# Mixture of experts in float32: tokens held in the array, or weights held in the array

## The chip, the cores and the metric

The kernel runs on one core of a Trainium2 chip. A core has TensorE (matrix products, with a separate instruction that loads the operand held in the array), VectorE, ScalarE, GpSimd and SyncE, which all run side by side and meet at semaphores, and 16 DMA engines that move data between the chip's main memory and the on-chip memory. TensorE writes its products to a small memory of banks (PSUM), from which VectorE and ScalarE read. The metric is the time of one execution on the device in microseconds (us), median of several runs. All data is float32.

## What is computed

Four layers run one after the other over an image batch `x` of shape (2, 128, 56, 56), each added to its input: agent attention, a 3x3 convolution, a mixture of experts over patches, and a pair of recurrent (Mamba) blocks. Only the third is touched:

```
xp = patches of the normalized x          # 1568 tokens of d = 512
probs = softmax(xp @ router_w)            # 8 experts
topv, topi = top_k(probs, 2)              # the two best, shares sum to 1
for e in range(8):
    h = xp @ w1[e]                        # w1[e]: 512 x 2048
    val, g = split(h, 2)                  # 1024 each
    he = val * sigmoid(g)
    out = out + gate[:, e:e+1] * (he @ w2[e])   # w2[e]: 1024 x 512
```

The kernel computes an expert only for the tokens that chose it.

## The kernel before, in words

**Routing.** `PatchExperts.route` finds the two experts of each token, sorts the 3136 pairs by expert, and pads each expert's pairs to whole tiles of 128 slots (`SLOTS`). The tokens lie in main memory as rows of 512 (`xd`). For the inputs shown here 28 tiles come out. `whom` holds the token of each slot, `whose` the expert of each tile, `share` the weight of each slot.

**One tile.** `PatchExperts.run` (line 1298) works through the tiles `j`. `gather(j)` fetches the tile's 128 token rows with an indirect DMA from GpSimd's queue into `xr` (four buffers). `up_weights` and `down_weights` (lines 1314 and 1319) bring the expert's two matrices, 4 MB and 2 MB, through SyncE's queue, each into one of two buffers, used in turn.

`up(j, w1, xr)` (line 1327) turns the token rows: four transposes on TensorE into a PSUM bank (`xr_ps`, line 1331) and one copy by VectorE (`xs_c`, line 1333), so that the 512 features lie on partitions as four blocks of 128, with the 128 tokens along the free axis. Then the first layer: for each half `c` of the 1024 inner features and each part (1, the gate; then 0, the value) four matmuls accumulate over the four feature blocks (line 1341). The token block `xc[:, q, :]` is held in the array and 512 columns of the matrix stream past it, so a row of the result is a token:

```
nc.tensor.matmul(h_ps, xc[:, q, :], w1[:, q, f0 : f0 + 512], start=q == 0, stop=q == 3)
```

ScalarE takes the sigmoid of the gate (`sg`, line 1344), VectorE multiplies (`he`, line 1345).

`down(j, he, w2)` (line 1348) computes the second layer. It sums over the 1024 inner features, so these must lie on partitions: eight transposes turn `he` in two banks (`he_ps`, line 1354), ScalarE copies the first to `ht` (line 1357), VectorE the second (line 1359). Then eight matmuls with 512 streamed columns accumulate `o_ps` (line 1362), ScalarE scales each row by its share (`ot`, line 1364) and sends it to `os` in main memory (line 1365).

**Order of the work.** The loop emits `up` of a tile before `down` of the tile before, and a scheduler with the pools' buffers as its limits decides each engine's final order. On TensorE a tile then reads: `xr` transposes, first four `he` transposes of the tile before, 16 matmuls of `h`, other four `he` transposes, eight matmuls of `o` of the tile before. PSUM has four buffers for `h`, two for the transposes (`xr_ps` and `he_ps` share them) and two for `o`. SyncE's queue is in order: the second-layer matrix for tile `j + 2` waits for `o` of tile `j`, and behind it stands the first-layer matrix for tile `j + 3`. The first 25 tiles are unrolled; for the rest a switch on the number of further tiles has one branch for each number, and three tiles are run there.

**Around it.** `combine` (line 1394) gathers each token's two result rows once the last `os` has landed, turns them and adds them to `x`; the recurrent stage starts from there.

Of the kernel before, what the change touches and what calls it, by code (L numbers as in the profile page):

```python
# [8 lines left out]
F32 = mybir.dt.float32  # L9
# [8 lines left out]
P = 128  # L18
# [991 lines left out]
SLOTS = 128  # L1010
# [3 lines left out]
class PatchExperts:  # L1014
# [283 lines left out]
    def run(self, wpool, work, ps):  # L1298
        net, nc, a = self.net, self.net.nc, self.net.a
        experts, hidden, toks = self.experts, self.hidden, self.toks  # L1300
        nj = hidden // P

        w1s = a["L2_conv_w1"].rearrange("e (c q) f -> e c q f", q=4)
        w2s = a["L2_conv_w2"].rearrange("e (j k) d -> e k j d", k=P)

        def expert(j):
            return bass.ds(nc.sync.value_load(self.whose[0:1, j : j + 1], min_val=0, max_val=experts - 1), 1)

        ups = [wpool.tile([P, 4, 2 * hidden], F32, name="w1", tag="w1") for _ in range(2)]
        downs = [wpool.tile([P, nj, 512], F32, name="w2", tag="w2") for _ in range(2)]  # L1310

        def up_weights(j, e):
            w1 = ups[j % 2]
            nc.sync.dma_start(w1, w1s[e].rearrange("o c q f -> (o c) q f"))
            return w1

        def down_weights(j, e):
            w2 = downs[j % 2]
            nc.sync.dma_start(w2, w2s[e].rearrange("o k j d -> (o k) j d"))
            return w2  # L1320

        def gather(j):
            xr = work.tile([SLOTS, 512], F32, name="xr", tag="xr", bufs=4)
            self.rows_of(xr, self.xd, self.whom[:, j : j + 1], toks)
            return xr

        def up(j, w1, xr):

            tp = ps.tile([P, 512], F32, name="xr_ps", tag="tr")
            for q in range(4):  # L1330
                nc.tensor.transpose(tp[:, q * P : (q + 1) * P], xr[:, q * P : (q + 1) * P], net.ident)  # L1331
            xc = work.tile([P, 4, SLOTS], F32, name="xs_c", tag="xs_c")
            nc.vector.tensor_copy(xc.rearrange("c q s -> c (q s)"), tp)
            he = work.tile([SLOTS, hidden], F32, name="he", tag="he")
            for c in range(2):
                parts = []
                for part in (1, 0):
                    h_ps = ps.tile([P, 512], F32, name="h_ps", tag="h", bufs=4)
                    f0 = part * hidden + c * 512
                    for q in range(4):  # L1340
                        nc.tensor.matmul(h_ps, xc[:, q, :], w1[:, q, f0 : f0 + 512], start=q == 0, stop=q == 3)  # L1341
                    parts.append(h_ps)
                sg = work.tile([SLOTS, 512], F32, name="sg", tag="sg")
                nc.scalar.activation(sg, parts[0], AF.Sigmoid)  # L1344
                nc.vector.tensor_mul(he[:, c * 512 : (c + 1) * 512], parts[1], sg)  # L1345
            return he

        def down(j, he, w2):
            ht = work.tile([P, nj, SLOTS], F32, name="ht", tag="ht")
            for c in range(2):  # L1350
                tp = ps.tile([P, 512], F32, name="he_ps", tag="tr")
                for i in range(4):
                    f0 = (4 * c + i) * P
                    nc.tensor.transpose(tp[:, i * P : (i + 1) * P], he[:, f0 : f0 + P], net.ident)
                to = ht[:, 4 * c : 4 * c + 4, :].rearrange("k j s -> k (j s)")
                if c == 0:
                    nc.scalar.copy(to, tp)  # L1357
                else:
                    nc.vector.tensor_copy(to, tp)
            o_ps = ps.tile([P, 512], F32, name="o_ps", tag="o")  # L1360
            for i in range(nj):
                nc.tensor.matmul(o_ps, ht[:, i, :], w2[:, i, :], start=i == 0, stop=i == nj - 1)  # L1362
            ot = work.tile([SLOTS, 512], F32, name="ot", tag="ot")
            nc.scalar.mul(ot, o_ps, self.share[:, j : j + 1])  # L1364
            nc.scalar.dma_start(self.os[j * SLOTS : (j + 1) * SLOTS, :], ot)


        more = nc.values_load(self.more[0:1, 0:1], min_val=0, max_val=TILES - self.fewest)
        last = None
        for j in range(self.fewest):  # L1370
            e = expert(j)
            w1, w2 = up_weights(j, e), down_weights(j, e)
            he = up(j, w1, gather(j))
            if last is not None:
                down(*last)
            last = (j, he, w2)
        e0 = expert(self.fewest)
        first = up_weights(self.fewest, e0), down_weights(self.fewest, e0)
        xrs = {j: gather(j) for j in range(self.fewest, self.fewest + 3)}
        before = last  # L1380
        for n in net.tc.Switch(more, TILES - self.fewest + 1):
            last = before
            for j in range(self.fewest, self.fewest + n):
                if j == self.fewest:
                    w1, w2 = first
                else:
                    e = expert(j)
                    w1, w2 = up_weights(j, e), down_weights(j, e)
                he = up(j, w1, xrs[j] if j in xrs else gather(j))
                down(*last)  # L1390
                last = (j, he, w2)
            down(*last)

    def combine(self, b, gathered, bank):
# [140 lines left out]
def mamba_pair(net, out, wts, combine):  # L1535
# [19 lines left out]
    with ExitStack() as ctx:  # L1555
# [443 lines left out]
        with tc.manual_schedule(engines={E.PE, E.Activation, E.DVE, E.Pool, E.SP}):  # L1999
            for n, _ in enumerate(arrive(0)):  # L2000
                if n == 1:

                    seen = work.tile([P, 1], F32, name="seen", tag="seen", bufs=1)
                    nc.scalar.copy(seen, net.xb(0, 0)[:, 0:1])
                    nc.scalar.preload_act_table_set(EXP_LN)
            second = arrive(1)
            first = min(agenda)
            for step in range(first, 0):
                run(step)
                for _ in range((0, 0, 0, 2, 0, 1, 1, 0, 1, 1, 1, 1, 0, 1, 1, 1)[step - first] if step - first < 16 else 1):  # L2010
                    next(second, None)
                fetch(step + 1)
            for _ in second:
                pass
        with tc.manual_schedule(engines={E.PE, E.Activation, E.DVE, E.Pool, E.SP}):
# [5 lines left out]
            for n, (h, u) in enumerate(units):  # L2021
                if n + 1 < len(units):
                    who, i = units[n + 1]
                    who.decay(i)
                fetch(n)
                if u % 2 == 0 and not (h.by_pool(u) and h.by_pool(u + 1)):
                    h.read_out(u)
                if u % 2 == 0 and n + 6 < len(units):
                    who, i = units[n + 6]
                    who.send_c(i // 2)  # L2030
                if n + 4 < len(units):
                    who, i = units[n + 4]
                    who.push(i)
                h.scan(u)
                if done:
                    done.pop().close()
                waiting.append((h, u))

                quota = 0 if u == 3 and n > 3 else 2 if u == 7 and n > 7 else 1
                for _ in range(quota):  # L2040
                    if len(waiting) > 3:
                        who, i = waiting.pop(0)
                        who.collect(i)
                        if i == UNITS - 1:
                            done.append(who)
                run(n)
# [4 lines left out]
            for step in range(len(units), max(agenda) + 1):  # L2051
                run(step)
                fetch(step + 1)
# [98 lines left out]
```

## Time and profile before

| | us |
|---|---|
| median of three runs (3051.7 to 3062.04) | 3058.73 |
| the profiled execution | 3043.85 |
| its span, first to last instruction | 3041.8 |
| experts: first `xr` transposes to last `ot` | 1027.3 to 1663.2 |
| one tile in the middle of that stage | 22.5 |

The profile is of one execution, and its times are set against that execution's own time. Of the groups of the page, these belong to the expert stage; the columns of the first three are line, engine, operation, names (written from read), shapes and count, then busy us and mean ns of one, then idle us of that engine before them with what ended it:

```profile
L1341 PE MATMUL h_ps<-w,xs_c 128*128 128x512 f32 x896 | 393.1, 597 | 10.3 <-issue 10.3
L1341 PEld LDWEIGHTS h_ps<-w,xs_c 128*128 128x128 f32 x896 | 168.9, 191 | 218.5 <-issue 202.7
L1362 PE MATMUL o_ps<-w,ht 128*128 128x512 f32 x448 | 197.2, 592 | 0.4 <-ACT ht L1357 0.4
w<-in_L_conv_w_dram SPq DMA_DIRECT2D x28, 4096.0 KB, 19.2
```

A shape such as `128*128 128x512` reads: the operand held in the array, then the streamed one (partitions x columns). PE is the matmul, PEld the load. A float32 matmul of the program shows as two matmul records with a load each: 28 tiles x 16 matmuls are 448, and 896 records stand on line 1341. The records overlap, so the time from start to start says more than the busy time. The last line is a DMA: the first layer's matrix, 28 times, 4 MB each, 19.2 us from issue to landing. A tenths row divides the span in 40 slices of 76 us.

### The profile page before, as it was taken

What the parts mean: (1) busy time and instruction counts of PE and PEld (TensorE: products, weight loads), DVE (VectorE), ACT (ScalarE), POOL (GpSimd) and SP (SyncE); (2) the same over time, 40 slices, a digit from 0 to 9 for tenths busy, and PEclk for the clock granted to TensorE, in tenths of its full rate; (3) what the DMA queues carried; (4) which work ended last, traced back from release to release, by engine and by line L of the source; (5) the groups of instructions that cost most, each with busy time, mean ns of one, the idle gap of its engine ahead of it and who ended that gap; (6) DMA issues with size and microseconds to landing.
All of it is one profiled execution on the core that took longest, in us unless ns stands there. A gap on an engine that the chain in (4) does not pass through costs nothing. (4 is left out here: it accounts for less than half of the span.)

```text
span 3041.8 us, 34551 instructions
## 1 busy us (share of the span) xinstructions
PE 2694.0 (89%) x12460; PEld 1070.0 (35%) x12460; DVE 2198.0 (72%) x1873; ACT 1866.8 (61%) x2970; POOL 1464.3 (48%) x801
## 2 busy tenths in 40 slices
PE   7999999999898799999998688888888888888874
PEld 3333333333235444444443333333333333333321
DVE  5978998999886311111111579999999999999996
ACT  5778888787651111011110478888888888988884
POOL 3000010010412000000000689999999999999995
PEclk9999999999999799999999789999999999999987
DMA  1000000000002678778784555665555665555560
GB/s 55 1 1 1 1 1 1 1 1 1 1 1 60 263 280 318 300 293 321 284 305 183 136 114 117 140 138 123 120 118 120 132 140 124 128 119 119 121 142 28
DMA packets 157915, 369.00 MB, mean 121 GB/s; under 512 B 25156, under 2 KB 114980, under 8 KB 154132
## 3 DMA queue, kind: packets, MB, share of 16 engines
q1 hardware_dynamic: 135744, 339.30, 38.7%
q0 software_dynamic: 5520, 15.62, 1.6%
q10 hardware_dynamic: 16452, 11.61, 1.2%
q8 instruction: 102, 1.67, 0.2%
q14 instruction: 97, 0.79, 0.1%
HBM read 297.89 MB, written 17.20 MB: 104 GB/s over the span
## 5 line engine op out<-in xcount | busy, mean ns | idle before, releaser
L1843 POOL TENSOR_TENSOR dBu<-dtu,Bs 128x896 f32<-128x896 f32 x448 | 935.9, 2146 | 16.5 <-DMA dtu<-sp_u 14.9
L1862 DVE TENSOR_TENSOR_SCAN h<-dA,dBu 128x896 f32<-128x896 f32 x448 | 881.9, 2008 | 26.1 <-ACT dA L1832 20.4
L620 ACT ACTIVATE ex<-sc 128x896 f32<-128x896 f32 (+1 forms) x700 | 602.7, 917 | 124.5 <-PE sc L617 113.3
L1884 PE MATMUL y<-h,both 128*64 128x448 f32 x1792 | 467.0, 613 | 86.5 <-POOL h L1871 80.0
L627 DVE TENSOR_TENSOR ex_sum<-ex_sum,ex 128x1792 f32<-128x1792 f32 (+1 forms) x238 | 492.7, 2070 | 35.2 <-ACT ex L620 21.2
L617 PE MATMUL sc<-q,k 32*128 32x448 f32 (+1 forms) x2800 | 403.5, 587 | 3.6 <-ACT ex L620 2.9
L1341 PE MATMUL h_ps<-w,xs_c 128*128 128x512 f32 x896 | 393.1, 597 | 10.3 <-issue 10.3
L1873 DVE TENSOR_TENSOR h<-h,c_ps 128x1792 f32<-128x1792 f32 (+1 forms) x168 | 326.6, 1944 | 27.6 <-ACT c_ps L1850 10.5
L635 PE MATMUL av<-ex,va 128*32 128x448 f32 (+1 forms) x2800 | 334.3, 552 | 0.1
L582 POOL TENSOR_TENSOR a_e<-a_e,a_inv 112x784 f32<-112x784 f32 x14 | 41.6, 2974 | 583.1 <-ACT ex L620 394.5
L1832 ACT ACTIVATE dA<-dt,f_A 128x448 f32<-128x448 f32 x448 | 282.7, 636 | 60.6 <-DVE h L1862 45.3
L1345 DVE TENSOR_TENSOR he<-h_ps,sg 128x512 f32<-128x512 f32 x56 | 38.5, 691 | 381.5 <-PE h_ps L1341 344.5
L1832 ACT ACTIVATE dA<-dt,b_A 128x448 f32<-128x448 f32 x448 | 282.7, 635 | 33.0 <-DVE h L1862 23.6
L1289 POOL DMA_INDIRECT xr<-xd,whom x28 | 28.0, 1001 | 535.2 <-PE xr_ps L1331 494.7
L1871 POOL TENSOR_TENSOR h<-h,Cs 128x1792 f32<-128x1792 f32 (+1 forms) x70 | 254.3, 3633 | 6.9 <-issue 4.6
L1884 PEld LDWEIGHTS y<-h,both 128*64 128x64 f32 x1792 | 119.0, 147 | 362.7 <-issue 219.0
L1341 PEld LDWEIGHTS h_ps<-w,xs_c 128*128 128x128 f32 x896 | 168.9, 191 | 218.5 <-issue 202.7
L617 PEld LDWEIGHTS sc<-q,k 32*128 32x128 f32 (+1 forms) x2800 | 137.7, 181 | 230.0 <-issue 132.3
L1362 PE MATMUL o_ps<-w,ht 128*128 128x512 f32 x448 | 197.2, 592 | 0.4 <-ACT ht L1357 0.4
L1344 ACT ACTIVATE sg<-h_ps 128x512 f32<-128x512 f32 x56 | 33.4, 597 | 256.5 <-PE h_ps L1341 256.5
L1364 ACT ACTIVATE ot<-o_ps,share 128x512 f32<-128x512 f32 x28 | 19.3, 688 | 278.9 <-PE o_ps L1362 278.9
L625 DVE TENSOR_TENSOR ex_sum<-ex 128x1792 f32<-128x1792 f32 x56 | 114.4, 2043 | 54.5 <-ACT ex L620 54.4
(336 smaller groups left out, 3082.6 us busy)
## 6 DMA issues: line engine op xcount, KB each, us to landing
w<-in_L_conv_w_dram SPq DMA_DIRECT2D x28, 4096.0 KB, 19.2
w<-in_L_conv_w_dram SPq DMA_DIRECT2D x28, 2048.0 KB, 10.2
Bs<-far SPq DMA_DIRECT2D x56, 896.0 KB, 8.7
Cs<-far SPq DMA_DIRECT2D x448, 112.0 KB, 3.0
dtu<-sp_u SPq DMA_DIRECT2D x108, 224.0 KB, 3.9
dt<-dt SPq DMA_DIRECT2D x108, 224.0 KB, 5.1
os<-ot ACTq DMA_DIRECT2D x28, 256.0 KB, 7.6
xd<-xt SPq DMA_DIRECT2D x14, 224.0 KB, 2.7
```

Source lines behind the costliest of these rows:

```text
L617: nc.tensor.matmul(sc[:size, j, :BLK], self.m.k[rows, at : at + size], self.q[rows, :], start=True, stop=True)
L620: nc.scalar.activation(ex[:size, 2 * g : 2 * g + 2, :], sc[:size, :, :BLK], AF.Exp, scale=scale)
L627: nc.vector.tensor_add(self.total[g][:size], self.total[g][:size], ex[:size])
L635: nc.tensor.matmul(self.av[rows, :BLK], self.m.va[:size, i, rows], self.ex[i][:size, h, :], start=i == 0, stop=i == STEPS - 1,)
L1341: nc.tensor.matmul(h_ps, xc[:, q, :], w1[:, q, f0 : f0 + 512], start=q == 0, stop=q == 3)
L1362: nc.tensor.matmul(o_ps, ht[:, i, :], w2[:, i, :], start=i == 0, stop=i == nj - 1)
L1832: nc.scalar.activation(self.dA[u][:, r * BLK : (r + 1) * BLK], self.dt2[:, m, r, :], AF.Exp, scale=self.w.A[:, j, 2 * m + r : 2 * m + r + 1],)
L1843: nc.gpsimd.tensor_tensor(self.dBu[u], self.dtu2[:, m], self.B[:, j, :].unsqueeze(1).to_broadcast(shape), ALU.mult)
L1862: nc.vector.tensor_tensor_scan(hf, af, bf, 0.0, ALU.mult, ALU.add)
L1871: nc.gpsimd.tensor_tensor(h4, h4, self.C[j].unsqueeze(1).to_broadcast(shape), ALU.mult)
L1873: nc.vector.tensor_tensor(h4, h4, self.c_ps[:, :BLK].unsqueeze(1).to_broadcast(shape), ALU.mult)
L1884: nc.tensor.matmul(self.y[r * H : (r + 1) * H, m, :BLK], both, self.hc[j][:, m, r, :], start=False, stop=j == PAIRS - 1)
```

## The change

The operands of the first layer trade places. A block of 128 columns of the matrix is held in the array, and the tile's 128 tokens stream past it; one matmul gives 128 inner features on partitions with the tokens along the free axis. Four such blocks share a PSUM bank, so the sigmoid and the product still work on 128 x 512. The product is written directly to `ht` in the form that the second layer reads, and `down` no longer turns anything: eight transposes and two copies per tile go. The number of first-layer matmuls rises from 16 to 64 per tile.

```diff
-            he = work.tile([SLOTS, hidden], F32, name="he", tag="he")
+            ht = work.tile([P, nj, SLOTS], F32, name="ht", tag="ht")
             for c in range(2):
                 parts = []
                 for part in (1, 0):
                     h_ps = ps.tile([P, 512], F32, name="h_ps", tag="h", bufs=4)
-                    f0 = part * hidden + c * 512
-                    for q in range(4):
-                        nc.tensor.matmul(h_ps, xc[:, q, :], w1[:, q, f0 : f0 + 512], start=q == 0, stop=q == 3)
+                    for i in range(4):
+                        f0 = part * hidden + (4 * c + i) * P
+                        for q in range(4):
+                            nc.tensor.matmul(
+                                h_ps[:, i * SLOTS : (i + 1) * SLOTS],
+                                w1[:, q, f0 : f0 + P],
+                                xc[:, q, :],
+                                start=q == 0,
+                                stop=q == 3,
+                            )
                     parts.append(h_ps)
-                sg = work.tile([SLOTS, 512], F32, name="sg", tag="sg")
+                sg = work.tile([P, 4 * SLOTS], F32, name="sg", tag="sg")
                 nc.scalar.activation(sg, parts[0], AF.Sigmoid)
-                nc.vector.tensor_mul(he[:, c * 512 : (c + 1) * 512], parts[1], sg)
-            return he
-
-        def down(j, he, w2):
-            ht = work.tile([P, nj, SLOTS], F32, name="ht", tag="ht")
-            for c in range(2):
-                tp = ps.tile([P, 512], F32, name="he_ps", tag="tr")
-                for i in range(4):
-                    f0 = (4 * c + i) * P
-                    nc.tensor.transpose(tp[:, i * P : (i + 1) * P], he[:, f0 : f0 + P], net.ident)
                 to = ht[:, 4 * c : 4 * c + 4, :].rearrange("k j s -> k (j s)")
-                if c == 0:
-                    nc.scalar.copy(to, tp)
-                else:
-                    nc.vector.tensor_copy(to, tp)
+                nc.vector.tensor_mul(to, parts[1], sg)
+            return ht
+
+        def down(j, ht, w2):
             o_ps = ps.tile([P, 512], F32, name="o_ps", tag="o")
```

The callers hand `ht` on in place of `he`. In the order as built, a tile on TensorE then reads: `xr` transposes, one matmul of `o` of the tile before, 64 matmuls of `h`, the other seven of `o`; at the start of the stage the `xr` transposes of the first four tiles stand ahead of the first `h`, and `o` is split in other places for the first four tiles.

More of the change, by code (lines that the diff above doesn't have):

```diff
@@ L1372, in run @@
             w1, w2 = up_weights(j, e), down_weights(j, e)
-            he = up(j, w1, gather(j))
+            ht = up(j, w1, gather(j))
             if last is not None:
                 down(*last)
-            last = (j, he, w2)
+            last = (j, ht, w2)
         e0 = expert(self.fewest)
@@ L1388, in run @@
                     w1, w2 = up_weights(j, e), down_weights(j, e)
-                he = up(j, w1, xrs[j] if j in xrs else gather(j))
+                ht = up(j, w1, xrs[j] if j in xrs else gather(j))
                 down(*last)
-                last = (j, he, w2)
+                last = (j, ht, w2)
             down(*last)
```

## The prediction

> **What bounds the kernel now.** I read the busy-time slices of the page first, to see where the experts lie and who is busy there; then the busy times by stretch; then the timeline of one tile, for the step that is late in each place; then rows elsewhere in the same trace that already do what the change will do.
>
> ```profile
> PE   7999999999898799999998688888888888888874
> PEclk9999999999999799999999789999999999999987
> DMA  1000000000002678778784555665555665555560
> ```
>
> ```profile
> 1200.00:1300.00 100.00, 98.03 (x268) 45.92 (x268) 11.38 (x17) 11.74 (x19) 4.98 (x5) 1.00 0.74 287
> ```
>
> Slices 14 to 22 are the experts (the first transpose at 1027.3 us, the last scaled output at 1663.2). The second fence is a stretch of 100 us: busy time and instructions of TensorE's matmuls, its loads, VectorE, ScalarE and GpSimd, then granted clock, DMA share and GB/s. From 1200 to 1300 the matmuls are busy 98 of 100 us at the full clock (1.00), VectorE and ScalarE about 11, the DMA engines 74%. So the stage lasts as long as TensorE's stream. A busy matmul row is no proof of that, as records overlap, so I went by start times:
>
> ```profile
> 1203.68 0.60 PE L1331 MATMUL xr_ps<-ident,xr 128*128 128x128 f32 x4
> 1204.11 0.60 PE L1354 MATMUL he_ps<-ident,he 128*128 128x128 f32 x4
> 1204.31 0.69 DVE L1333 COPY xs_c<-xr_ps 128x512 f32<-128x512 f32 x1 [6.38 <-PE xr_ps L1331]
> 1205.11 13.97 PE L1341 MATMUL h_ps<-w,xs_c 128*128 128x512 f32 x32 [0.39 <-issue]
> 1218.91 0.60 PE L1354 MATMUL he_ps<-ident,he 128*128 128x128 f32 x4
> 1219.35 7.03 PE L1362 MATMUL o_ps<-w,ht 128*128 128x512 f32 x16
> 1226.22 0.60 PE L1331 MATMUL xr_ps<-ident,xr 128*128 128x128 f32 x4
> ```
>
> One tile, from xr to xr, takes 22.54 us: xr 0.43, first he transposes and the wait for the token copy xs_c 1.00, h 13.80, second he transposes 0.44, o 6.87. Each float32 matmul shows as two records, "passes" below: 32 for h, 16 for o, 429 ns apart. Only xr to h holds idle time: the xs_c copy ends 1.32 us after xr begins and h starts at 1.43.
>
> [...] loads of 190 ns stand between passes that start every 429 ns. [...] The router's sums (line 1116: 112 columns loaded, 8 streamed) show 13 loads in 1.36 us at 178 ns each, so (1.36 - 0.18) / 12 = 98 ns apart[...]. [...] this trace shows 0.50 from 1010 to 1020 us.
>
> **The change, part by part.** Only the expert stage differs: the built order of every engine outside it is the same but for semaphore names.
>
> *The first layer* becomes 64 matmuls, 128 passes of 128 columns in place of 32 passes of 512. The streamed columns are the same, but each pass now has a 128-column load of its own. The price is the spacing of such pairs, which attention's values show, in full float32, as do the fuse products:
>
> ```profile
> 29.37 2.81 PEld L548 LDWEIGHTS v_ps<-wv,xn 128*128 128x128 f32 x24
> 29.54 2.84 PE L548 MATMUL v_ps<-wv,xn 128*128 128x128 f32 x24
> ...
> 1854.45 0.60 PE L1627 MATMUL fuse_ps<-f_out_t,zs 128*112 128x128 f32 x4
> ...
> 1854.89 0.60 PE L1627 MATMUL fuse_ps<-b_out_t,zs 128*112 128x128 f32 x4
> ```
>
> Values: (2.84 - 0.273) / 23 = 111.6 ns, the last record being 273 ns. Fuse: (1854.89 - 1854.45) / 4 = 110 ns, 109 over longer groups, with only 112 columns loaded. So loads and streams run side by side and the longer sets the pace; with 128 columns it is the load[...]. I take 111.6: 128 x 0.1116 = 14.28 us, 0.48 more than now. Ends for the range: 109 (a stream alone) and 113.9, the spacing of the values' load records, (2.81 - 0.19) / 23.
>
> *The transposes go*: eight of he per tile, 0.87 us. Their two copies of 0.59 us (ScalarE) and 0.68 us (VectorE) go as well, worth nothing, since both engines are 88% idle here. VectorE's multiply, 0.69 us as before, now writes ht directly.
>
> *The hole between xr and h.* In the built order one second-layer matmul of the tile before (two passes, 0.86 us) now stands where four he transposes (0.44 us) stood, and seven follow h. h still starts 1.43 us after xr, because the xs_c copy sets that: xr ends at 0.43, o at 1.29, xs_c at 1.32, and the wait in front of h also holds back h's first load. What is late next is therefore the same copy, and nothing is queued behind it that others wait for. So xr to h stays 1.43, h is 14.28, and the other seven o matmuls 14 x 0.4294 = 6.01. Sum 21.72 us, 0.82 less per tile.
>
> *New waits.* o's first matmul waits for the multiply of the tile before, over 7 us old by then. The h groups wait on TensorE's own count for passes of the tile before, long done. ht has two buffers, and the multiply that reuses one comes a whole tile after its last reader. All at nothing.
>
> *Transfers.* SP issues the second layer's matrix when o of a tile ends, then the first layer's for three tiles on. That one takes 19.2 us to land (21.0 at most) from 0.76 us after o's end, and its h starts one period and 1.43 us after o's end: 23.97 us now, 23.15 after. Slack falls from 4.0 to 3.2 us, or 1.4 at the slowest landing. The gathers' queue is issued from xr as before.
>
> *Start of the stage.* The new order puts the first four tiles' transposes ahead of h of tile 0. The fourth gather is issued at 1024.09 and lands 7.7 us later, at 1031.8; with 1.0 us of slow transposes h starts at 1032.8 instead of 1030.48. It runs at the slow clock for 4 us as now. Followed through its loads (tile 1's matrix lands at 1047, tile 3's at about 1090 to 1092), tile 4's xr comes at 1112.65 against 1113.50: 0.85 less, three tiles' gain mostly spent on the late start, with the two xr-to-h holes of tiles 2 and 3 removed.
>
> *End of the stage.* Now xr of the last tile to its scaled output takes 1663.21 - 1632.08 = 31.13 us. After: xr 0.43, two o matmuls 1.72, h 14.28, six o 5.15, the last tile's eight 6.87 and 0.30 to the scaling, 28.75. That is 2.4 less; the last pair of transposes and their copy are bare today.
>
> Sum: 0.85 + 23 x 0.82 + 2.4 = 22.1 us. The recurrent stage that follows begins at the last output's gather, so it shifts whole. The profiled execution's 3043.85 us (span 3041.8) becomes 3021.8. The runs' median, 3058.73, stands 14.9 above it; less 22.1 it is 3036.6.
>
> **The rivals.** *The passes come slower than the pairs elsewhere show* (the slower one). Per tile 128 x p + 7.44 = 22.54 at p = 118.0 ns: beyond that the change loses. The known runs have at most 24 passes in a row; here 128 follow, 256 instructions in 14.3 us, 17.9 per us. The longest dense evidence is in attention:
>
> ```profile
> 878.00:887.00 9.00, 9.00 (x84) 2.47 (x80) 8.72 (x6) 7.25 (x9) 0.00 (x0) 1.00 0.01 2
> 300.00:320.00 20.00, 19.56 (x160) 6.96 (x160) 19.56 (x20) 15.92 (x21) 0.00 (x0) 1.00 0.00 1
> ```
>
> That is 164 in 9 us, 18.2 per us, but over 20 us only 16, bounded there by the matmuls themselves. Were 16 the supply, p would be 125 ns, h 16.0 us, the tile 23.44: 0.90 x 28 = 25 us more, 3084. For it: nothing shows 18 held for 14 us. Against: the values' 49 instructions in 2.6 us. Chance 0.05.
>
> *The array's clock drops.* The inverse-slot products show dense passes that never woke it:
>
> ```profile
> 1007.30 12.02 PEld L1275 LDWEIGHTS inv<-room 112*128 112x128 f32 x56 [3.46 <-issue]
> 1007.33 12.18 PE L1275 MATMUL inv<-room 112*128 112x64 f32 x56 [3.29 <-DVE tile_f L1250]
> ```
>
> (12.18 - 0.42) / 55 = 214 ns a pass at clock 0.50. There 64 columns stream per 128-column load, so half the time is idle[...]. If it fell all the same, h would take 128 x 0.214 = 27.4 us and the tile 34.8, which is 12.3 more than now: 28 times that is 344 us, some 3400. Loads that don't overlap would cost about the same[...]; the values' rows exclude that. Both 0.03.
>
> *The matrices arrive late.* If the shorter period stretched landings by more than the 3.2 us of slack, to 22.4 and up to 23.2, the period would stay near 22.5 and the time near 3056. Against: 6.29 MB land in 19.8 us, 318 GB/s, while 1015 to 1020 us shows 439 GB/s. Chance 0.04.
>
> **How the numbers follow.** The forecast has 0.88. Its own range: 109 ns is 128 x 28 x 2.6 ns = 9 us less, 113.9 ns is 8 us more, so 3027 to 3045; the three runs before lie 7 below and 3 above their median, which adds about 5 each way: 3022 to 3050. The rivals above it are 0.12, which may stay out. What can be told from no change is 0.3%, 9 us. Faster 0.88, same 0.04, slower 0.08.
>
> **What would show it.** Right: h as 128 passes in about 14.3 us at clock 1.00; xr to xr 21.7; no he rows; one o matmul between xr and h, and h still 1.43 after xr; the last output's scaling about 22 us earlier; the recurrent stage as long as before. Wrong: passes over 118 ns apart; clock under 1 inside h; h waiting for a matrix; or xr to h grown, if the wait for xs_c comes later than the copy's present place.

## The result and the profile after

| | before | after |
|---|---|---|
| median of the first comparison (6 runs each) | 3061.5 | 3039.5 |
| ratio, 95% interval | | 0.9937 [0.9916, 0.9959] |
| the profiled execution, its span | 3043.85, 3041.8 | 3034.5, 3032.4 |
| first `xr` transposes to last `ot` | 635.87 | 615.89 |
| one tile in the middle | 22.55 | 21.81 |
| last `ot` to the end of the span | 1378.6 | 1387.4 |

The medians fell by 22.0 us, where 22.1 were forecast. The two profiled executions, for which 22.1 were forecast too, differ by only 9.4, because the stage behind the experts, whose code is the same, was 8.8 us longer in the second. The experts themselves became 20.0 us shorter, and that is the number to explain.

The busy times from 1200 to 1300 us after the change, columns as before:

```profile
1200.00:1300.00 100.00, 100.00 (x699) 82.45 (x698) 9.68 (x14) 9.04 (x15) 4.99 (x5) 1.00 0.81 316
```

TensorE is still the bound: 100 of 100 us, at the full clock. The loads now fill 82 us instead of 46, and VectorE and ScalarE have less to do. One tile by start times, from the timeline (start, length, engine, line, what, and in brackets the idle time before with its releaser):

```profile
1200.12 0.60 PE L1331 MATMUL xr_ps<-ident,xr 128*128 128x128 f32 x4
1200.55 1.02 PE L1359 MATMUL o_ps<-w,ht 128*128 128x512 f32 x2
1200.76 0.69 DVE L1333 COPY xs_c<-xr_ps 128x512 f32<-128x512 f32 x1 [5.69 <-PE xr_ps L1331]
...
1201.55 14.53 PE L1342 MATMUL h_ps<-xs_c,w 128*128 128x128 f32 x128
...
1215.91 6.17 PE L1359 MATMUL o_ps<-w,ht 128*128 128x512 f32 x14
...
1221.93 0.60 PE L1331 MATMUL xr_ps<-ident,xr 128*128 128x128 f32 x4
```

xr to h is 1.43 us as before, but two passes of the second layer (0.86) now lie in it instead of four transposes (0.44). h takes 14.36, the other 14 passes 6.02. Set against before, h costs 0.56 us more, the eight transposes of 0.87 are gone, and the bare part of the hole shrinks from 0.56 to 0.14, so by 0.42. Together that is 0.73 less, of 0.74 measured (22.547 - 21.809, means over 23 tiles).

The two ends of the stage, in the same timeline, show what no middle tile shows:

```profile
1029.06 1.09 PE L1331 MATMUL xr_ps<-ident,xr 128*128 128x128 f32 x4 [8.01 <-DMA xr<-xd,whom]
...
1034.15 15.42 PE L1342 MATMUL h_ps<-xs_c,w 128*128 128x128 f32 x128
...
1054.56 14.45 PE L1342 MATMUL h_ps<-xs_c,w 128*128 128x128 f32 x128
1068.85 4.46 PE L1359 MATMUL o_ps<-w,ht 128*128 128x512 f32 x10
...
1614.50 0.60 PE L1331 MATMUL xr_ps<-ident,xr 128*128 128x128 f32 x4
...
1614.76 1.29 DVE L1353 TENSOR_TENSOR ht<-h_ps,sg 128x512 f32<-128x512 f32 x2 [20.73 <-PE o_ps L1359]
...
1615.51 1.98 PE L1359 MATMUL o_ps<-w,ht 128*128 128x512 f32 x4 [0.40 <-DVE ht L1353]
...
1637.03 1.29 DVE L1353 TENSOR_TENSOR ht<-h_ps,sg 128x512 f32<-128x512 f32 x2 [20.38 <-PE o_ps L1359]
...
1637.77 7.13 PE L1359 MATMUL o_ps<-w,ht 128*128 128x512 f32 x16 [0.84 <-DVE ht L1353]
...
1644.95 0.69 ACT L1361 ACTIVATE ot<-o_ps,share 128x512 f32<-128x512 f32 x1 [7.29 <-PE o_ps L1359]
```

At the start h of the first tile begins 5.09 us after the first xr (3.14 before); the second tile's h, which waits for nothing, takes 1068.85 - 1054.56 = 14.29 us. At the end VectorE's multiply waits 20 us for `o`, and TensorE then waits for the multiply. The `o` that ends the first of these waits is that of the tile just before: its last pass comes right ahead of the xr at 1614.50, while `o` of two tiles back had ended by 1592.70.

The wait on VectorE is not new. In the last two tiles of the kernel before, the multiply stood in the same way:

```profile
1625.46 1.29 DVE L1345 TENSOR_TENSOR he<-h_ps,sg 128x512 f32<-128x512 f32 x2 [14.60 <-PE he_ps L1354]
```

There it ended with the `he` transposes of the tile just before, which came right behind h, and TensorE had `o` to go on with. New is that it lasts to the end of `o` and that TensorE is held up by it.

### The profile page after: what moved, and what is told of

The parts are those of the page before. It is cut to its first block, busy times and chain, and to the rows that moved or that the text cites. A ratio compares the mean times of both kernels' runs of the same rounds, so it can differ in the third digit from the quotient of the medians.

```text
span 3032.4 us, 39344 instructions
## 1 busy us (share of the span) xinstructions
PE 2681.1 (88%) x14924; PEld 1275.2 (42%) x14924; DVE 2182.4 (72%) x1845; ACT 1848.6 (61%) x2942; POOL 1472.2 (49%) x801
## 5 line engine op out<-in xcount | busy, mean ns | idle before, releaser
L627 DVE TENSOR_TENSOR ex_sum<-ex_sum,ex 128x1792 f32<-128x1792 f32 (+1 forms) x238 | 492.5, 2069 | 35.3 <-ACT ex L620 21.3
L1342 PEld LDWEIGHTS h_ps<-xs_c,w 128*128 128x128 f32 x3584 | 403.7, 192 | 19.6 <-ACT ot L1361 17.7
L1342 PE MATMUL h_ps<-xs_c,w 128*128 128x128 f32 x3584 | 407.4, 276 | 0.0
L1353 DVE TENSOR_TENSOR ht<-h_ps,sg 128x512 f32<-128x512 f32 x56 | 38.5, 691 | 418.0 <-PE h_ps L1342 365.8
L1361 ACT ACTIVATE ot<-o_ps,share 128x512 f32<-128x512 f32 x28 | 19.2, 687 | 244.0 <-PE o_ps L1359 244.0
L625 DVE TENSOR_TENSOR ex_sum<-ex 128x1792 f32<-128x1792 f32 x56 | 114.4, 2042 | 54.6 <-ACT ex L620 54.5
## 6 DMA issues: line engine op xcount, KB each, us to landing
w<-in_L_conv_w_dram SPq DMA_DIRECT2D x28, 4096.0 KB, 20.4
```

The costliest lines, as they stand in the source:

```text
L627: nc.vector.tensor_add(self.total[g][:size], self.total[g][:size], ex[:size])
L1342: nc.tensor.matmul(h_ps[:, i * SLOTS : (i + 1) * SLOTS], w1[:, q, f0 : f0 + P], xc[:, q, :], start=q == 0, stop=q == 3,)
```

## The experiments

### The transposes alone

```diff
-            ht = work.tile([P, nj, SLOTS], F32, name="ht", tag="ht")
-            for c in range(2):
...
+            ht = he.rearrange("s (j k) -> s j k", k=P)
```

From the kernel before: the gated rows go unturned into the second layer.

> The kernel before, with the gated inner rows taken directly as the operand held for the second layer; the eight transposes of a tile and their two copies are left out, so the second layer's result is another one. First layer as before: 32 passes of 512 columns. If the prediction's two terms are both right in size, the transposes' side is 8 x 0.109 = 0.87 us and the growth of the first layer is separate from it: a tile takes 1.43 (xr to h) + 13.80 + 14 x 0.4294 = 21.24 us, which is 1.30 less than before (0.87 of transposes, 0.43 of a second-layer matmul that moves into the hole), 28 x 1.30 = 36 us less in all, ratio about 0.988; against the changed kernel, 0.57 us per tile or 16 us less is then the price of the 128 loads per tile. Rival, transfers or the token copy become the limit: the tile stays at 21.8 or above, ratio 0.994 or more.

Measured: ratio 0.9876 [0.9858, 0.9894], first xr to last `ot` 600.6 us, 35.3 less than before. The timeline:

```profile
1215.24 0.60 PE L1331 MATMUL xr_ps<-ident,xr 128*128 128x128 f32 x4
1215.67 1.02 PE L1352 MATMUL o_ps<-w,he 128*128 128x512 f32 x2
1216.67 13.97 PE L1341 MATMUL h_ps<-w,xs_c 128*128 128x512 f32 x32
1230.47 6.17 PE L1352 MATMUL o_ps<-w,he 128*128 128x512 f32 x14
1236.48 0.60 PE L1331 MATMUL xr_ps<-ident,xr 128*128 128x128 f32 x4
```

The tile is 21.24 us, as the sum said. So the transposes and the hole are worth 1.30 us a tile when nothing is paid for them, and the change's own loads give 0.57 of it back (21.81 - 21.24).

### What sets the pace of the passes

Three kernels from the changed one. First, 112 columns held, not 128, with the later steps narrowed to these 112 rows (the diffs from here on show the lines that matter; `...` marks what is left out):

```diff
-                                w1[:, q, f0 : f0 + P],
+                                w1[:, q, f0 : f0 + 112],
...
```

> The changed kernel with 112 columns of the first matrix held instead of 128 (one eighth of the inner features is left out); as many passes, each still streaming 128 tokens. If the load of 128 columns sets the 112.2 ns between passes, the spacing falls to the 109 ns of the stream: h 128 x 0.109 = 13.95 us, 0.41 less, the tile 21.4. If a fixed cost per instruction sets it (256 instructions in 14.4 us), it stays at 112 ns, h 14.36, tile 21.8.

```profile
1055.94 14.14 PE L1342 MATMUL h_ps<-xs_c,w 128*112 128x128 f32 x128
1069.92 4.46 PE L1359 MATMUL o_ps<-w,ht 112*128 112x512 f32 x10
```

In this timeline the second tile's h takes 13.98 us, 109.2 ns a pass, against 111.6 with 128 columns. The middle tile is 21.47 us. The load sets the pace in the changed kernel, with the stream 2.4 ns behind it; the number of instructions is the same in both, so it is not what binds.

Second, blocks of 64 columns held and 64 tokens streamed:

```diff
-                    for i in range(4):
-                        f0 = part * hidden + (4 * c + i) * P
+                    for i in range(8):
+                        f0 = part * hidden + (8 * c + i) * 64
...
-                                w1[:, q, f0 : f0 + P],
-                                xc[:, q, :],
+                                w1[:, q, f0 : f0 + 64],
+                                xc[:, q, :64],
...
```

> The changed kernel with blocks of 64 columns held and 64 tokens streamed, 256 passes per tile (half of the tokens is left out, and the second layer's rows are mixed). If passes are paced by load and stream alone, 64 columns cost about half of 111.6: 56 to 58 ns a pass, h 14.3 to 14.9 us, about 34 matmul and load instructions per us. If the supply of instructions has a limit not far above the 17.9 per us of the changed kernel (the prediction's slower rival), a pass takes 100 ns or more, h 25.6 us or more, and the stage grows by 300 us or more.

```profile
1034.02 16.23 PE L1342 MATMUL h_ps<-xs_c,w 128*64 128x64 f32 x256
...
1210.09 15.14 PE L1342 MATMUL h_ps<-xs_c,w 128*64 128x64 f32 x256
1225.16 6.27 PE L1359 MATMUL o_ps<-w,ht 64*128 64x512 f32 x14
```

The first line is from the first tile of the stage and will be needed below. In the middle tile 256 passes take 15.07 us: 58.9 ns each, 512 instructions in 15.07 us or 34 per us. That is twice the rate of the changed kernel, so the prediction's limit of supply is not near. (The stage is longer than after the change, 22.9 us a tile; part is h, part the second layer, whose passes with 64 rows came 443 ns apart instead of 429. Why they did was not tried.)

Third, the tokens streamed in two halves, with a full load for each:

```diff
-                        for q in range(4):
...
+                        for t in (0, 64):
+                            for q in range(4):
+                                nc.tensor.matmul(
+                                    h_ps[:, i * SLOTS + t : i * SLOTS + t + 64],
+                                    w1[:, q, f0 : f0 + P],
+                                    xc[:, q, t : t + 64],
...
```

> The changed kernel with the tokens streamed in two halves of 64, so that each 128-column load serves 64 streamed columns: 256 passes per tile. Load-bound at full clock: 112 ns a pass, h 28.7 us, tile about 36.2, 400 us more in all. If the clock falls to half because the array streams only half of the time, as the rival of the prediction had it from the inverse-slot rows: 214 ns a pass, h 55 us, tile about 62, 1130 us more, with a granted clock of 0.5 in the stage.

Measured: one run of 3469.66 us; the middle tile 36.10, its h 28.61 or 111.8 ns a pass at the full clock. So where loads are longer than streams, the loads alone count. But the first tile behaved otherwise. Its timeline, then its busy times with the clock in the third column from the right:

```profile
1035.37 54.72 PE L1343 MATMUL h_ps<-xs_c,w 128*128 128x64 f32 x256
1089.87 5.71 PE L1360 MATMUL o_ps<-w,ht 128*128 128x512 f32 x10
1095.42 28.69 PE L1343 MATMUL h_ps<-xs_c,w 128*128 128x64 f32 x256
```

```profile
1036.00:1046.00 10.00, 10.00 (x49) 10.00 (x48) 0.00 (x0) 0.00 (x0) 0.84 (x1) 0.50 0.97 399
...
1076.00:1086.00 10.00, 10.00 (x49) 10.00 (x49) 0.00 (x0) 0.60 (x1) 0.00 (x0) 0.50 0.00 0
1090.00:1095.00 5.00, 5.00 (x11) 2.14 (x11) 1.29 (x2) 0.00 (x0) 0.00 (x0) 0.77 0.85 315
1096.00:1106.00 10.00, 10.00 (x92) 10.00 (x91) 0.00 (x0) 0.60 (x1) 0.00 (x0) 1.00 0.49 210
```

From a start at the low clock the same passes ran at 0.50 for all of 54.5 us (213 ns each). The clock came up during the ten passes of 512 columns behind them (0.77 in the mean of 1090 to 1095, 1.00 from 1096 to 1106); after that the half-filled stream kept the full clock. Both theories were right, each for one state: such passes didn't wake the clock, and they didn't lose it (1.00 from 1100 to 2070 us).

In the changed kernel, with 128 columns streamed, the clock was up about 2 us into the first h (0.50 from 1034 to 1036, 0.96 from 1036 to 1038). It is not the 64 columns as such that keep the clock down: with 64 columns held and 64 streamed the first h took 16.15 us (1034.02 to 1050.17) and the second 15.08, 1.07 less; in the changed kernel the two are 15.25 and 14.29, 0.96 apart, and here 54.50 and 28.53. What sets the sleeping case apart in these runs is that a pass streams half as many columns as its load holds. So do the inverse-slot products (64 columns streamed, 128 held), which stayed at 0.50 through all of their 12 us.

### How much is order

The changed kernel with the next tile's transposes and copy ahead of the second layer, and a third buffer for `ht`:

```diff
-            ht = work.tile([P, nj, SLOTS], F32, name="ht", tag="ht")
+            ht = work.tile([P, nj, SLOTS], F32, name="ht", tag="ht", bufs=3)
...
-            ht = up(j, w1, gather(j))
+            ht = up(j, w1, xc)
+            if j + 1 < self.fewest:
+                xc = turn(gather(j + 1))
...
```

> The changed kernel, with the four token transposes and the copy of the next tile placed after the first layer of this tile, ahead of its predecessor's second layer, and a third buffer for ht. If the 1.43 us from xr to h is only the wait for the copy, it is covered by the eight second-layer matmuls: a tile takes 0.43 + 14.36 + 6.87 = 21.67 us against 21.81, 4 us less in all; and if the 0.7 and 0.8 us holes of the last tiles come from ht having two buffers, xr of the last tile to its scaled output falls by about 1.7 us: together 5 to 6 us below the changed kernel, ratio against before about 0.991 to 0.992. Rival, the holes of the last tiles have another cause (the order of the queues): a wait of VectorE's multiply for o stays in the last branch and only 3 to 4 us are gained. Rival, the tile is bound by the transfers: stays at 21.8.

```profile
1204.04 14.45 PE L1344 MATMUL h_ps<-xs_c,w 128*128 128x128 f32 x128
1218.33 0.60 PE L1330 MATMUL xr_ps<-ident,xr 128*128 128x128 f32 x4
...
1225.64 14.46 PE L1344 MATMUL h_ps<-xs_c,w 128*128 128x128 f32 x128
```

The timeline has no hole: 21.60 us a tile, 0.07 less than expected, because h falls to 14.29. In a middle tile of the changed kernel the wait in front of h also holds back its first load, which starts only 0.03 us ahead of the first pass (1594.10 and 1594.13). Where h waits for nothing the load is 0.43 us ahead (1616.90 and 1617.33 in the changed kernel's last tile), and here it is so in every middle tile. The experts take 611.0 us; ratio 0.9918 [0.9902, 0.9934].

Then the kernel before with its layout kept and the order alone changed: token transposes ahead of the second layer, the eight `he` transposes (split off as `flip`) ahead of the next first layer.

```diff
+            if last is not None:
+                last = flip(*last)
-            he = up(j, w1, gather(j))
+            he = up(j, w1, xc)
+            if j + 1 < self.fewest:
+                xc = turn(gather(j + 1))
...
-        before = last
+        before, ahead = flip(*last), turn(xrs[self.fewest])
...
```

> The kernel before with its layout and its transposes kept, and only the order changed: the next tile's token transposes and copy stand ahead of the second layer, and the eight he transposes ahead of the next first layer, so that no copy is waited for. If the hole from xr to h is worth what the timelines say, a tile takes 0.43 + 6.87 + 0.87 + 13.80 = 21.97 us, 0.57 less than before, and the run is about 15 us shorter, ratio about 0.995: then most of the change's 20 us is to be had by order alone, and against the turned layout in the same order (21.60) the layout itself is worth 0.87 - 0.49 = 0.38 us a tile. Rival, the hole is not the copy but the matrices or the transposes' own waits: the tile stays at 22.4 or more and the ratio at 0.998 or more.

Measured: ratio 0.9992 [0.9983, 1.0002], a miss. The timeline shows a middle tile of 21.91 us as forecast, and the loss in one place, where the program branches on the number of further tiles:

```profile
1571.89 0.38 SPq L1319 DMA_DIRECT2D w<-in_L_conv_w_dram  x1
...
1573.11 0.66 PE L1330 MATMUL xr_ps<-ident,xr 128*128 128x128 f32 x4 [0.38 <-ACT ht L1359]
...
1579.92 0.34 SPq L1314 DMA_DIRECT2D w<-in_L_conv_w_dram  x1
...
1581.52 8.72 PE L1343 MATMUL h_ps<-w,xs_c 128*128 128x512 f32 x15 [7.75 <-issue]
```

SyncE's last transfer before the branch and its first one in it lie 8.0 us apart, and did so in the kernel before as well (8.1, 1587.12 to 1595.21). TensorE shows the same gap only here: its last instructions ahead of the branch waited for a copy (`<-ACT ht`). h of that tile then took 15.85 us instead of 13.74: its loads came 0.85 us apart until 1585, and 0.43 from 1585.8 on. What fills the gap on either engine, and why it stays hidden on TensorE in the kernel before, was not shown.

The experts took 628.1 us, 7.8 less than before, while the medians differ by 2.3 only; the runs of before in that session had a median of 3051.6, ten below the other sessions', and what that came from is open.

So the same again, with the transposes of the tile that crosses moved into the branch (the diff is against the run just shown):

```diff
-        before, ahead = flip(*last), turn(xrs[self.fewest])
+        before = last
...
-            last, xc = before, ahead
+            last = before
+            if n:
+                xc = turn(xrs[self.fewest])
...
```

> As the kernel before with its order alone changed, but the tile that crosses the switch keeps its transposes inside the branch, so that nothing that waits stands ahead of the branch. If the 7.75 us hole and the 2.1 us of slow clock after it at the switch ate the gain of the first try, the steady tile is 21.91 us again, no hole is left at the switch, and the experts take about 628.1 - 10 = 618 us from the first xr to the last scaled output, 18 less than before: ratio 0.994. If the stage stays near 628, the loss had another cause. Against the changed kernel (615.9) it would then be 2 us longer, against the changed kernel with the order ahead (611.0) 7 us: that last is the turned layout's own worth.

```profile
1573.70 0.60 PE L1330 MATMUL xr_ps<-ident,xr 128*128 128x128 f32 x4
1574.14 0.60 PE L1356 MATMUL he_ps<-ident,he 128*128 128x128 f32 x4
1575.14 0.66 PE L1356 MATMUL he_ps<-ident,he 128*128 128x128 f32 x4 [0.40 <-DVE xs_c L1332]
1575.63 13.90 PE L1343 MATMUL h_ps<-w,xs_c 128*128 128x512 f32 x32
```

The 7.75 us are gone from the timeline, only 0.40 are bare. The changed kernel with the order ahead has transposes in front of the branch too, but none that wait, and loses 0.98 us there. The experts take 620.0 us and the ratio is 0.9937 [0.9924, 0.9949]. Beside it on the same chip the changed kernel and the one with the order ahead, each once more:

> The changed kernel, unchanged, profiled a second time and timed beside the two reordered ones: tile 21.81 us, experts 615.9 us from the first xr to the last scaled output, ratio 0.993 to 0.994 against before if the 22 us stand; 0.996 or more if part of the first comparison was scatter of the other stages.

> The changed kernel with the next tile's transposes ahead, repeated for a direct comparison: experts 611.0 us, 4.9 less than the changed kernel, so a ratio 0.0016 below the changed kernel's beside it; the rival, that this gain is lost outside the experts as the first profile's later stage suggested (1399.6 us against 1387.4), gives the same ratio for both.

| same session | first xr to last `ot` | tile | median | ratio to before |
|---|---|---|---|---|
| before (12 runs) | 635.9 (other session) | 22.55 | 3062.2 | |
| order alone | 620.0 | 21.91 | 3043.2 | 0.9937 [0.9924, 0.9949] |
| the change | 616.6 | 21.81 | 3042.3 | 0.9935 [0.9921, 0.9950] |
| the change, order ahead | 610.7 | 21.60 | 3032.7 | 0.9903 [0.9889, 0.9917] |

The old layout with a better order does what the change does, within the intervals. The order ahead keeps its gain in the whole time: 0.0032 below the change where 0.0016 was expected, and the stage itself is 5.9 us shorter; the rest of the 9.5 us between those two medians is not accounted for. In the same order the turned layout is worth 21.91 - 21.60 = 0.31 us a tile, 9.3 us over the stage (the third `ht` buffer is in this too). The last row is the fastest of this table.

### The wait at the end

The changed kernel with a third buffer for `ht`, nothing else:

```diff
-            ht = work.tile([P, nj, SLOTS], F32, name="ht", tag="ht")
+            ht = work.tile([P, nj, SLOTS], F32, name="ht", tag="ht", bufs=3)
```

> The changed kernel with a third buffer for ht and nothing else. If the two buffers make the multiply of the last tiles wait for o of two tiles before (20.7 and 20.4 us on VectorE, of which 0.7 and 0.8 us are bare on TensorE), no wait for o is left on the multiply, xr of the last tile to its scaled output takes 28.8 us instead of 30.45, and the experts from first xr to last scaled output about 614.6 us instead of 615.9 and 616.6. If the scheduler's order at the end of the branch makes the holes, 30.4 stays. The steady tile is 21.81 either way.

```profile
1615.35 0.60 PE L1331 MATMUL xr_ps<-ident,xr 128*128 128x128 f32 x4
...
1616.78 14.53 PE L1342 MATMUL h_ps<-xs_c,w 128*128 128x128 f32 x128
1631.14 13.04 PE L1359 MATMUL o_ps<-w,ht 128*128 128x512 f32 x30
```

No multiply waits for `o` any more, and the last tile goes through without a hole: 28.87 us from xr to the scaled output at 1644.22, and 614.7 for the stage. The number of buffers was the cause; the second profile of the change has both waits again (20.73 and 20.38 us). The expectation has `o` of two tiles before as what the multiply waited for; by the times it was `o` of the tile just before (see the two ends above), as if only one of the two buffers were left there. In the middle tiles no multiply waits for `o`. Why the second buffer is not free at the end stays open: the traces leave buffer numbers out.

### Transfers

The changed kernel with two of the four feature blocks:

```diff
-                        for q in range(4):
+                        for q in range(2):
...
```

> The changed kernel with two of the four feature blocks summed (half of the first layer is left out), transfers as before: TensorE needs 21.81 - 64 x 0.1116 = 14.7 us a tile. If the matrices come at most at the 316 to 318 GB/s seen in the stage, 6.29 MB take 19.8 us and the tile is 19.8 to 20: then only 1.8 us per tile is left to any further gain on TensorE. If they can come at the 439 GB/s of the stage's beginning, 14.3 us, the tile falls to 14.7 to 15.

```profile
1213.62 0.60 PE L1331 MATMUL xr_ps<-ident,xr 128*128 128x128 f32 x4
1215.79 7.38 PE L1342 MATMUL h_ps<-xs_c,w 128*128 128x128 f32 x64 [1.58 <-DMA w<-in_L_conv_w_dram]
...
1229.88 0.60 PE L1331 MATMUL xr_ps<-ident,xr 128*128 128x128 f32 x4
```

```profile
1200.00:1300.00 100.00, 91.12 (x517) 66.53 (x517) 11.88 (x18) 11.29 (x18) 5.99 (x6) 0.98 1.02 417
```

Neither number came. The timeline shows a tile of 16.26 us whose h waits for the matrix (16.40 in the mean of 18 tiles); the busy times show the DMA engines full (1.02) at 417 GB/s. So 316 GB/s is what TensorE's pace asks for and no limit; the floor of the transfers lies at 16.4 us, 5.4 below the changed kernel's tile.

### The stage that follows

> The kernel before, unchanged, profiled a second time. The recurrent stage, from the last scaled output of the experts to the end, took 1378.6 us in the first profile of before and 1387.4 after the change, with the same instructions in it; in the four experiments so far it took 1387.6 to 1399.6. If these 8.8 us are scatter of that stage between executions, it takes 1385 to 1400 us here and the whole run is near 3060; if the change costs it 9 us, it takes 1379 again, while the experts take 635.9 either way.

| last `ot` to the end of the span | first profile | second profile |
|---|---|---|
| before | 1378.6 | 1394.2 |
| the change | 1387.4 | 1387.7 |
| the change, order ahead | 1399.6 | 1392.2 |

It was scatter: the kernel before took 1394.2 us there in its second profile (span 3059.4), with 635.9 for the experts both times. The same instructions spread over 21 us between executions, and the first profile of before was its shortest.

## Why the prediction was right

**The bound.** Right: TensorE stays full at clock 1.00, and the transfers have 5.4 us a tile to spare.

**The pass.** 111.6 ns was exact where h waits for nothing (14.29 us / 128, here and in the reordered kernels), and the load was rightly named as the longer of the two: with 112 columns held the pass fell to 109.2. In the middle tile h takes 14.36 us. The prediction saw that the wait in front of h holds back its first load, but took the 111.6 for all passes; the 13.80 of before has the same 0.06 in it (13.74 in the reordered one). That term was 0.08 us a tile too small, 1.9 us over 23 tiles.

**Transposes and hole.** Both right: 0.87, and 1.43 from xr to h, set by the copy. The experiments add what the prediction didn't say: over half of the 0.74 us (0.42) comes from what now stands in the hole, and an order without a hole has it with the old layout too.

**New waits: "All at nothing".** Wrong, and the step that failed. It reasoned from the middle tile, in which the multiply that reuses an `ht` buffer comes a whole tile after its last reader. In the last two tiles it comes behind `o` of the tile just before. The trace of before showed such a wait already, 14.60 us for `he`, at no cost: `he` was read for the last time right behind h. `ht` is now held from the multiply to the end of `o`. That left the last tile's xr-to-h with 0.68 us bare where 0.14 is usual, and 1.00 us bare ahead of its own `o` (1636.77 to 1637.77, by start times). The end took 30.45 us, not 28.75; with a third buffer it is 28.87.

**Start.** h of the first tile came 1.95 us later, 2.3 forecast. The stretch from the first xr to xr of tile 4 shrank by 2.33 us (86.16 to 83.83) instead of 0.85. About 1.1 us of the difference come from the clock, which woke about 2 us into h (0.96 from 1036 to 1038) and not 4 (before: 0.50 from 1030 to 1034, 0.67 from 1034 to 1035). That was luck as far as the runs show: the two kernels with the order alone changed have the same instructions up to there, and their first h took 14.62 and 15.84 us.

**Transfers.** Right: no h of a middle tile waited for a matrix. The landing went from 19.2 to 20.4 us, inside the slack of 3.2.

**Sum.** 2.33 + 23 x 0.738 + 0.68 = 20.0 us against 22.1: 1.5 more at the start, mostly by luck, 1.9 less in the middle, 1.7 less at the end. That the first medians differ by 22.0, so close to 22.1, is partly chance: the second comparison gave 3062.2 - 3042.3 = 19.9.

**"Shifts whole"** holds within the scatter, but the scatter is larger than the 5 us each way taken from three runs. The profiled execution, put at 3021.8 us, took 3034.5.

**The rivals.** Slow supply is refuted at 34 instructions per us; loads in series by 111.6 ns (the load and then the stream would take some 221 ns, an estimate from the 111.6 of a pass that the load paces and the 109.2 of one with 112 columns held); late matrices by the spare time. The clock rival did not happen, and the reason given against it stood its test: with half as many columns streamed as held the first tile stayed at 0.50, with as many streamed as held it did not, at 128 columns as at 64.

## What to carry to other kernels

Before an operation is taken out of a hole, ask what fills the hole without it: here over half of the gain was a wait that got covered, and moving the transposes earlier covered it without a new layout. When a result is written earlier than the buffer it replaces, count its buffers again at the last iterations, not only in the middle, and look there for waits that cost nothing yet: a longer hold can make them cost. Where a program branches, keep instructions that wait from standing directly ahead of the branch: TensorE stood for 7.75 us here with them there, and for 0.40 with them inside.

## What the hardware showed unexpectedly

- Dense passes of 64 streamed columns per 128-column load left the clock at 0.50 for 54.5 us, with TensorE's record full (10.00 us of the 10 from 1076 to 1086). So busy by the record was not enough. The stretch that the prediction gives at 0.50, 1010 to 1020 us, is another such case: the inverse-slot products fill 9.5 of its 10 us. With as many columns streamed as held (128 or 64) the first h took 0.96 to 1.64 us longer than the second, in seven traces, so the clock came up some 1.9 to 3.3 us into it, an estimate from these differences at half the pace. No run tried a ratio of streamed to held columns between a half and one, and what holds the clock down at a half was not shown. Once up, the clock stayed at 1.00 through the 28.6 us of half-filled passes in every later tile (1.00 from 1100 to 2070 us).
- At the branch SyncE's two transfers lie 7.9 to 8.1 us apart in seven traces (before, the change twice, and four experiments); TensorE stood for 7.75 us there only in the one where its last instructions ahead of the branch had to wait.
- The recurrent stage spread over 21 us between executions of identical instructions, as much as the whole change is worth.
